# Reordering the first three stages of an eight-layer kernel: weights ahead of x, squares on ScalarE, weight copies on GpSimd, the next layer's weights behind the first rows

## The chip, the cores and the metric

The kernel runs on one core of one Trainium2 chip. The metric is the device time of one execution in microseconds (us), as the median of several runs. A core has a matmul engine (TensorE, PE in the profile; its weight loads are PEld), a vector engine (VectorE, DVE), a scalar and activation engine (ScalarE, ACT), a general engine (GpSimd, POOL) and a queue engine (SyncE, SP). Each runs its own instructions in program order and waits on semaphores for the others. SP, ACT and POOL ask for DMA transfers; an instruction that asks for one takes its place in that engine's order.

## The reference, cut to what matters

Eight layers, attention and feed-forward in turn, each `x = layernorm(x + layer(x))` on x of 8 × 256 × 256, fp32. The change touches the first three:

```python
# layer 0, attention: rotary positions, 16 query heads of 16, 4 key heads
q, k, v = x @ wq, x @ wk, x @ wv            # causal softmax(q k') v @ wo
...
# layer 0, feed-forward: 32 experts of 128 in 4 groups; each token takes 2 groups, 8 experts
scores = sigmoid(x @ gate_w.T)
... # the 2 best groups by (scores + bias), the 8 best experts in them
cw = normalised scores of those * 2.5
x_lat = x @ fc1_w.T
h = relu2(x_lat @ w1[e].T) * cw[:, e]       # relu2(x) = relu(x) ** 2
routed = sum_e(h @ w2[e].T) @ fc2_w.T
shared = relu2(x @ shared_up_w.T) @ shared_down_w.T
return shared + routed
...
# layer 1, attention: 16 heads of 128; q and k are normalised (rms) and scaled by gq and gk
```

## The kernel before, in words

The layers are eight phases in a row: attn0, ffn0, attn1, ffn1, attn2, ffn2, attn3, ffn3. x stays on chip in eight tiles X0 to X7 (256 tokens each) and transposed in four blocks xT of 512 tokens. In the first phases the order of instructions on PE, DVE, ACT and POOL is the order of the program (a hand-made schedule, `manual_schedule(engines=COMPUTE)` in `tile_layers`): python generators for pieces of work are stepped in turn, and each `yield` marks a place where another piece may be put in between. In ffn0, SP is not part of that order before the change.

**Start.** `Model.__init__` asks for the identity and for X0 to X7, even ones on SP and odd ones on ACT (L74 to L77), then for the mask `tri` (L80). `attn0_load` (L229) asks on SP, behind them, for wq in two halves, wk, wv, wo, then the rotary tables tq, ck, sk and delta. The first product of attn0 is x·wk in `project` (L279), behind the transposes of X (L145); VectorE makes kh from it with ck and sk (L288).

**attn0** (L241). A loop over eight batches (L478): maxima, spread, weights and finish of each, with pieces of other work put in at `fill` (L455 to L466): the projections of the coming block, and `beside`, the sort of ffn0's first token group, which starts at batch `NB - 2` of `NB = 8` (L488). Block 0 of ffn0's shared expert (`between`) fills the last batch.

**ffn0** (L1197). The tokens are two groups. `ffn0_sort` (L950) makes gate scores, the two groups of experts of each token, its place in a list sorted by expert group, and the eight weights, into the tile `lat` (L1036), and scatters the rows of `lat` by an indirect DMA on POOL (L929), 16 of them, into `lrows` in memory, two between `yield`s (L1040 to L1044). `ffn0_experts` (L1075) then takes 19 tiles of 128 rows a group: `fetch` loads two tiles `xg` from `lrows` (L1087, SP), `turn` copies the eight experts' first weights of that tile's expert group into `wc` (L1096 to L1101: an index read into ScalarE's register, then a copy of 128 × 1024) and transposes `xg` (L1103, copied as `xTg` by VectorE, L1105). `up` multiplies four experts (L1111), takes relu on ACT (L1116) and the square on POOL (`hg`, L1118); `down` multiplies with the second weights (L1128) and sums with the tokens' weights on DVE (`yg`, L1137 and L1139), and stores the tile (`louts`, L1141). Two halves make a tile: up of half s, then down of half s − 2. Meanwhile another generator is stepped once a half: for group 0 the sort of group 1, for group 1 `ffn0_combine` (L1156) of group 0, which gathers on POOL (L1167), adds, multiplies with fc2 (L1188), adds to x, and normalises (`normed`, L181; transposes of X in `norm_done`, L145).

Between attn0 and the tiles stand blocks 1 and 2 of the shared expert (`ffn0_shared`, L1046: up L1054, relu on ACT L1059, square on DVE L1060, down L1067, sum L1072); block 3 stands between the two groups' tiles. ffn0's second weights `f0_w2` are asked for as ffn0 begins (L1203; w_f_w in the profile), behind attn1's six weight loads of 1 MB (w_a_wq, w_a_wk, w_a_wv) and the two vectors gq and gk of 0.5 KB, which `open_weights` asks for on SP as the phase ffn0 opens.

**attn1** (L1247) first makes `gqk = gq * gk` on DVE (L1256), then works in units of a batch and four heads, its order written out in a list of `at(...)` calls; k's transposes (L1320) wait for its normalisation (L1295).

Of the kernel before, what the change touches and what calls it, by code (L numbers as in the profile page):

```python
# [18 lines left out]
P = 128  # L19
# [20 lines left out]
class Model:  # L40


    def __init__(self, ctx, tc, ins, out):
        self.tc, self.nc, self.ins, self.out = tc, tc.nc, ins, out
        nc = self.nc
        self.const = ctx.enter_context(tc.tile_pool(name="const", bufs=1, side="left"))
        self.small = ctx.enter_context(tc.tile_pool(name="small", bufs=4, side="left"))
        self.psum = ctx.enter_context(
            tc.tile_pool(name="psum", bufs=2, space=bass.MemoryType.PSUM)
        )  # L50
        self.n_ev = 0
# [26 lines left out]

        self.tri = c.tile([P, 2 * P], F32, name="tri")
        nc.scalar.dma_start(out=self.tri, in_=ins["c_tri"])  # L80
# [3 lines left out]
        for j in range(4):  # L84
            nc.vector.tensor_copy(self.maskA[:, j, :], self.tri[:, P:])
# [3 lines left out]
        nc.gpsimd.memset(self.nhalf, -0.5)  # L89


    def ps(self, tag):
        return self.psum.tile([P, 512], F32, tag=tag, name=f"ps_{tag}")
# [17 lines left out]
        else:  # L111
            self.nc.scalar.copy(out, in_)

    def load(self, pool, name, shape, split=1):
        t = pool.tile(list(shape), F32, name=f"w_{name}", tag=f"w_{name}", bufs=1)
        src = self.ins[name]
        if split == 1:
            self.nc.sync.dma_start(out=t, in_=src)
        else:
            step = shape[1] // split  # L120
            for i in range(split):
                s = slice(i * step, (i + 1) * step)
                self.nc.sync.dma_start(out=t[:, s], in_=src[:, s])
        return t

    def load_row(self, pool, name, n):
# [101 lines left out]

    def attn0_load(self, pool):  # L229
        return dict(  # L230
            wq=self.load(pool, "a0_wq", [P, 2, 512], split=2),
            wk=self.load(pool, "a0_wk", [P, 2, 256]),
            wv=self.load(pool, "a0_wv", [P, 2, 64]),
            wo=self.load(pool, "a0_wo", [P, 2, D]),
            tq=self.load(pool, "c_tq0", [P, T]),
            ck=self.load(pool, "c_ck0", [P, T]),
            sk=self.load(pool, "c_sk0", [P, T]),
            delta=self.load(pool, "c_delta", [P, 4]),
        )

    def attn0(self, w, act, start=False, beside=None, between=()):  # L241
# [236 lines left out]
        for b in range(NB):  # L478
            nxt = None
            if b == 0 or b % 2 == 1:  # L480
                drain()
                if (b + 3) // 2 < NBLK:
                    ahead.append(project((b + 3) // 2))
            if b + 1 < NB:
                nxt = maxima(b + 1)
            else:
                ahead.append(between)
            if b == NB - 2 and beside:  # L488
                sorting.append(beside)
# [12 lines left out]
            ends.append(finish(b))  # L502
            prev = nxt
# [446 lines left out]
    def ffn0_sort(self, w, g, act, keep, tag="a"):  # L950
# [87 lines left out]
            )  # L1038
        yield
        self.sorted0[g] = slots, expert  # L1040
        rows = self.scatter(self.lrows[g], slots, lambda t, k: lat[:, t, k, :])
        for i, _ in enumerate(rows):
            if i % 2 == 1:
                yield  # L1044

    def ffn0_shared(self, w, blk, act, tags=("hs", "relu"), bufs=2):  # L1046

# [3 lines left out]
        for m in range(4):  # L1051
            pu = self.ps("a" if m % 2 else "s")
            for c in range(2):
                nc.tensor.matmul(  # L1054
                    pu, w["up"][:, c, m * P : (m + 1) * P], xT[:, c, :],
                    start=(c == 0), stop=(c == 1),
                )
            relu = act.tile([P, BLK], F32, tag=tags[1], name="relu")
            nc.scalar.activation(relu, pu, AF.Relu)  # L1059
            nc.vector.tensor_tensor(hs[:, m, :], relu, relu, ALU.mult)  # L1060
            yield
        for i in range(2):
            y = self.ps("o").rearrange("p (t d) -> p t d", t=2)
# [11 lines left out]
    def ffn0_experts(self, w1, w2, g, act):  # L1075
# [17 lines left out]
        def turn(j):  # L1093
            if j % 2 == 0:
                fetch(j + 4)
            e = nc.scalar.value_load(expert[0:1, j : j + 1], min_val=0, max_val=3)  # L1096
            wc[j] = act.tile([P, 8, P], F32, tag="wc", name="wc", bufs=2)
            nc.scalar.copy(
                wc[j].rearrange("p e f -> p (e f)"),
                w1[:, bass.ds(e, 1), :].rearrange("p o f -> p (o f)"),  # L1100
            )  # L1101
            pt = self.ps("a")[:, :P]
            nc.tensor.transpose(pt, xg[j][:, :P], self.ident)  # L1103
            xT[j] = act.tile([P, P], F32, tag="xTg", name="xTg", bufs=3)
            nc.vector.tensor_copy(xT[j], pt)  # L1105

        def up(s):
            j, half = divmod(s, 2)
# [6 lines left out]
            relu = act.tile([P, BLK], F32, tag="rl", name="rl", bufs=3)  # L1115
            nc.scalar.activation(relu, ps, AF.Relu)  # L1116
            h[s] = act.tile([P, BLK], F32, tag="hg", name="hg", bufs=3)
            nc.gpsimd.tensor_tensor(h[s], relu, relu, ALU.mult)  # L1118

        def down(s):  # L1120
            j, half = divmod(s, 2)
# [34 lines left out]
    def ffn0_combine(self, w, g, keep):  # L1156
# [6 lines left out]
        for t in range(2 * n + 1):  # L1163
# [32 lines left out]

    def ffn0(self, w, act, keep, temp, sort, start=False):  # L1197

# [13 lines left out]
        for blk in (1, 2):  # L1212
            for i, _ in enumerate(self.ffn0_shared(w, blk, act)):
# [33 lines left out]
    def attn1(self, w, act, beside, then, start=False):  # L1247
# [179 lines left out]
        for n in range(len(units) + 2):  # L1427
# [28 lines left out]
            at(0, "values", 1)  # L1456
            at(0, "turned", "q", 1)
            at(1, "weights", 1)
            if 0 <= n - 2 and units[n - 2].g == 3:
# [599 lines left out]
def tile_layers(ctx: ExitStack, tc: tile.TileContext, ins, out, phases):  # L2059
# [21 lines left out]
        stack[i] = (s, load(pool, *args))  # L2081

    open_weights(0)
    left = []
    for i, name in enumerate(phases):
        m.last = i == len(phases) - 1
        with tc.tile_pool(name=f"act{i}", bufs=2, side=sides[i % 2]) as act:
            if not m.last and name != "attn1":
                open_weights(i + 1)
            w, start = stack[i][1], i == 0  # L2090
            with tc.manual_schedule(engines=COMPUTE) if name in MANUAL else ExitStack():
                if name == "attn0":
                    beside, between = None, iter(())
                    if not m.last:
# [2 lines left out]
                        between = m.ffn0_shared(wn, 0, act, ("qT", "kh0"), bufs=3)  # L2097
                    m.attn0(w, act, start, beside, between)
                elif name == "ffn0":
                    left = m.ffn0(w, act, kept[i], m.temp, left, start=start)  # L2100
                elif name == "attn1":

                    def then(i=i):
# [140 lines left out]
```

## Time and profile before

| | us |
|---|---|
| median of 3 runs (lowest to highest) | 2634.99 (2633.07 to 2637.95) |
| the profiled execution | 2582.73 |
| its span | 2580.8 |
| PE busy in the span | 2234.2 (87%) |
| DVE, ACT, POOL busy | 1454.7, 1019.0, 935.0 |
| attn0, until its last product | 0 to about 274.7 |
| end of attn0 to the first up of ffn0's tile 0 | 274.7 to 318.7 |
| ffn0's tiles of group 0 | 318.7 to 424.1 |
| block 3 of the shared expert | 424.1 to 438.3 |
| ffn0's tiles of group 1 | 438.3 to about 538 |
| attn1's first unit, until its loop is full | about 538 to 560 |

The profile is of one execution. A group's line reads: line of the kernel, engine, operation, output <- input by the program's names, shapes, count | busy time, mean ns of one | idle time of the engine just before these instructions, and what released it. A line of the timeline has start, duration, engine and operation, and in square brackets how long the engine stood idle before it and who released it; SPq is a DMA that SP asks for. In the view by stretches the columns are explained in its head line; PEclk is the granted TensorE clock as a share of full speed. In the profile `w_a_`, `w_f_` and `w_c_` are weights of attention, feed-forward and constants.

### The profile page before, as it was taken

Reading aid. Unit: us, or ns where it says so; the run is one execution under the profiler, and the core shown is the slowest. Engines: PE = TensorE matmul, PEld = TensorE weight load, DVE = VectorE, ACT = ScalarE, POOL = GpSimd, SP = SyncE. Lnnn points to the kernel's source line nnn. Section 1 sums busy time; section 2 is a strip of 40 time slices with the busy share of each in tenths; the row PEclk is TensorE's granted clock in tenths of the full one; section 3 lists DMA queues with packets and bytes.
Section 4 is the critical chain, followed back from the end, with each engine's and each line's share of the span. In section 5 each row is a group of like instructions: output and inputs, shape, how many; then the busy total and the mean of one; then the engine's idle time right before and its main releaser. Section 6 shows DMA issues by size and latency. Waiting matters only on the chain. (4 is left out here: it accounts for less than half of the span.)

```text
span 2580.8 us, 36064 instructions
## 1 busy us (share of the span) xinstructions
PE 2234.2 (87%) x12016; PEld 1518.6 (59%) x12016; DVE 1454.7 (56%) x3651; ACT 1019.0 (39%) x2909; POOL 935.0 (36%) x1637
## 2 busy tenths in 40 slices
PE   8998788889999999999999999998878777668890
PEld 4554577856666665666664555555555554457780
DVE  3565485755445445445455444556888878635453
ACT  1223143435435445445442112221666756634450
POOL 1222246544334233233313221000566656824415
PEclk9998899999999999999999999999989988789995
DMA  5000401110000100000080011002000000156653
GB/s 155 1 1 1 156 24 43 33 46 5 3 5 8 46 1 1 1 1 1 1 271 1 1 49 50 1 0 89 13 2 1 1 1 15 40 137 195 194 182 97
DMA packets 92306, 120.74 MB, mean 47 GB/s; under 512 B 9757, under 2 KB 79582, under 8 KB 91102
## 3 DMA queue, kind: packets, MB, share of 16 engines
q1 hardware_dynamic: 82702, 96.15, 11.8%
q0 software_dynamic: 8192, 21.11, 2.6%
q8 instruction: 100, 1.64, 0.3%
q10 hardware_dynamic: 1232, 1.18, 0.1%
q14 instruction: 80, 0.66, 0.1%
HBM read 67.53 MB, written 50.88 MB: 46 GB/s over the span
## 5 line engine op out<-in xcount | busy, mean ns | idle before, releaser
L1363 POOL TENSOR_SCALAR p<-p,rs 128x128 f32<-128x128 f32 (+1 forms) x256 | 104.2, 424 | 293.1 <-DVE rs L1361 282.1
L1353 ACT ACTIVATE p<-ps_s,nm,rq 128x128 f32<-128x128 f32 (+1 forms) x256 | 127.9, 506 | 148.4 <-DVE nm L1351 148.3
L137 POOL TENSOR_SCALAR rsq<-bnmv 128x2 f32<-128x2 f32 x64 | 13.7, 213 | 456.7 <-DVE bnmv L175 449.2
L1281 ACT ACTIVATE sq<-ps_a 128x512 f32<-128x512 f32 x126 | 76.0, 603 | 226.4 <-PE ps_a L1273 210.4
L638 ACT ACTIVATE e<-ps_a,nm 128x128 f32<-128x128 f32 (+1 forms) x256 | 105.8, 435 | 111.2 <-DVE nm L635 92.2
L1282 DVE TENSOR_REDUCE ssk<-sq 128x4 f32<-128x512 f32 x64 | 43.8, 686 | 174.5 <-ACT sq L1281 174.5
L680 POOL TENSOR_SCALAR v<-e,r,nmd 128x128 f32<-128x128 f32 (+1 forms) x256 | 135.9, 542 | 10.0
L1273 PE MATMUL ps_a<-w_a_wq,xT 128*128 128x512 f32 x256 | 123.4, 605 | 10.8 <-DVE k L1295 8.3
L697 PE MATMUL ps_t<-ident,v 128*128 128x128 f32 x384 | 70.3, 320 | 68.2 <-DVE qT L576 31.4
L672 DVE SCALAR_TENSOR_TENSOR e<-e,c 128x128 f32<-128x128 f32 (+1 forms) x256 | 106.2, 465 | 34.8 <-POOL c L659 34.6
L1946 PE MATMUL ps_a<-w_f_gup,xTg 128*128 x504 | 111.7, 346 | 14.7 <-DVE xTg L1940 6.8
L1273 PE MATMUL ps_a<-w_a_wv,xT 128*128 128x512 f32 x256 | 120.5, 593 | 0.0
L1273 PE MATMUL ps_a<-w_a_wk,xT 128*128 128x512 f32 x248 | 116.5, 593 | 0.0
L1282 DVE TENSOR_REDUCE ssq<-sq 128x4 f32<-128x512 f32 x64 | 43.9, 686 | 128.8 <-ACT sq L1281 128.8
L1401 PE MATMUL ps_o<-w_a_wo,attT 128*128 128x256 f32 x512 | 111.8, 379 | 0.0
L1139 DVE SCALAR_TENSOR_TENSOR yg<-ps_t,xg,yg 128x128 f32<-128x128 f32 x266 | 93.1, 350 | 26.5 <-PE ps_t L1128 17.9
L1118 POOL TENSOR_TENSOR hg<-rl 128x512 f32<-128x512 f32 x76 | 79.0, 1043 | 79.9 <-ACT rl L1116 79.6
L638 ACT ACTIVATE e<-ps_s,nm 128x128 f32<-128x128 f32 (+1 forms) x256 | 106.8, 453 | 0.0
L1401 PEld LDWEIGHTS ps_o<-w_a_wo,attT 128*128 128x128 f32 x512 | 96.8, 190 | 12.7
L1128 PE MATMUL ps_t<-w_f_w,hg 128*128 x608 | 87.2, 290 | 18.2 <-POOL hg L1118 8.4
L697 PEld LDWEIGHTS ps_t<-ident,v 128*128 128x128 f32 x384 | 50.5, 164 | 88.7 <-POOL nmd L677 44.9
L1340 PE MATMUL ps_s<-kT,qT 128*128 128x256 f32 (+1 forms) x512 | 100.1, 329 | 0.0
(402 smaller groups left out, 6142.5 us busy)
## 6 DMA issues: line engine op xcount, KB each, us to landing
rows<-zero SPq DMA_DIRECT2D x42, 384.0 KB, 4.4
xg<-rows SPq DMA_DIRECT2D x42, 384.0 KB, 3.8
outs<-yg SPq DMA_DIRECT2D x42, 384.0 KB, 4.2
w_f_gup<-in_f_gup SPq DMA_DIRECT2D x8, 768.0 KB, 10.0
w_f_w<-in_f_w SPq DMA_DIRECT2D x8, 512.0 KB, 10.4
w_f_down<-in_f_down SPq DMA_DIRECT2D x8, 384.0 KB, 9.2
w_f_up<-in_f_up SPq DMA_DIRECT2D x5, 512.0 KB, 7.2
lrows<-zero SPq DMA_DIRECT2D x12, 204.0 KB, 5.4
```

The costliest lines, as they stand in the source:

```text
L638: nc.scalar.activation(e[:, s, j * nk : (j + 1) * nk], sc[s][:, j, :], AF.Exp, bias=nm[:, s, j : j + 1], scale=1.0, accum_out=sums[:, s, j ...
L672: nc.vector.scalar_tensor_tensor(d[:, s, h, :], u.e[:, s, h, 1, :], u.c[:, s, h : h + 1], d[:, s, h, :], ALU.mult, ALU.add,)
L680: nc.gpsimd.tensor_scalar(u.v[:, s, h, :], d[:, s, h, :], u.r[:, s, h, 0:1], nm[:, s, h : h + 1], ALU.mult, ALU.add,)
L697: nc.tensor.transpose(ps[:, s, c, :], x, self.ident)
L1139: nc.vector.scalar_tensor_tensor(acc[j], y, c, acc[j], ALU.mult, ALU.add)
L1273: nc.tensor.matmul(ps, self.xt(u.b, t, c), w[which][:, c, u.cols], start=(c == 0), stop=(c == 1),)
L1282: nc.vector.tensor_reduce(out, sq, AX.X, ALU.add)
L1340: nc.tensor.matmul(sc[:, j, :], u.qT[:, h0 + j, qc * P : (qc + 1) * P], u.kT[:, h0 + j, 0:nk], start=(j == 0), stop=False,)
L1353: nc.scalar.activation(u.p[qc][:, h0 + j, :], sc[:, j, :], AF.Exp, bias=nm[:, j : j + 1], scale=r[:, j : j + 1], accum_out=u.sums[qc][:, h ...
L1363: nc.gpsimd.tensor_scalar(u.p[qc][:, j, :], u.p[qc][:, j, :], ri[:, j : j + 1], 1.0, ALU.mult, ALU.mult,)
L1401: nc.tensor.matmul(y[:, t, :], attTs[b][:, h, t * P : (t + 1) * P], w["wo"][:, h, :], start=(h == 0), stop=(h == 15),)
L1946: nc.tensor.matmul(ps, xT[j][:, c, :], w["gup"][:, bass.ds(er[j], 1), c, :].rearrange("p o f -> p (o f)"), start=(c == 0), stop=(c == 1),)
```

## The change

At the start only X0 and X1 are asked for, then attn0's weights (wk first; ck, sk, tq on the ACT queue), then the mask and the rest of x. The sort of group 0 starts one batch earlier in attn0, and yields after each scatter. The squares of ffn0 (shared and experts) go to ACT, the copy `wc` with its index read to POOL, the copy `xTg` to ACT. `ffn0_combine` has one `yield` more for each batch. In ffn0 the sort of group 1 is made during block 2 of the shared expert instead of behind it; attn1's weights are asked for there too, by `then()`, behind the tile generator's first step; and SP is part of the written order in ffn0. In attn1 the first unit's two `values` (4 matmuls each) come earlier.

```diff
@@ Model.__init__
-        for b in range(NB):
-            (nc.sync if b % 2 == 0 else nc.scalar).dma_start(
-                out=self.X[b], in_=ins["x"][b].rearrange("(t p) d -> p t d", p=P)
-            )
+        self.load_x(0, 2)
...
+    def load_rest(self):
+
+        self.nc.scalar.dma_start(out=self.tri, in_=self.ins["c_tri"])
+        for j in range(4):
+            self.nc.vector.tensor_copy(self.maskA[:, j, :], self.tri[:, P:])
+        self.load_x(2, NB)
...
@@ attn0_load
         return dict(
+            wk=self.load(pool, "a0_wk", [P, 2, 256]),
+            ck=self.load(pool, "c_ck0", [P, T], eng=self.nc.scalar),
+            sk=self.load(pool, "c_sk0", [P, T], eng=self.nc.scalar),
             wq=self.load(pool, "a0_wq", [P, 2, 512], split=2),
-            wk=self.load(pool, "a0_wk", [P, 2, 256]),
+            tq=self.load(pool, "c_tq0", [P, T], eng=self.nc.scalar),
...
@@ attn0
-            if b == NB - 2 and beside:
+            if b == NB - 3 and beside:
                 sorting.append(beside)
@@ ffn0_sort
-        rows = self.scatter(self.lrows[g], slots, lambda t, k: lat[:, t, k, :])
-        for i, _ in enumerate(rows):
-            if i % 2 == 1:
-                yield
+        yield from self.scatter(self.lrows[g], slots, lambda t, k: lat[:, t, k, :])
@@ ffn0_shared
-            nc.vector.tensor_tensor(hs[:, m, :], relu, relu, ALU.mult)
+            nc.scalar.activation(hs[:, m, :], relu, AF.Square)
@@ ffn0_experts
-            e = nc.scalar.value_load(expert[0:1, j : j + 1], min_val=0, max_val=3)
+            e = nc.gpsimd.value_load(expert[0:1, j : j + 1], min_val=0, max_val=3)
...
-            nc.scalar.copy(
+            nc.gpsimd.tensor_copy(
...
-            nc.vector.tensor_copy(xT[j], pt)
+            nc.scalar.copy(xT[j], pt)
...
-            nc.gpsimd.tensor_tensor(h[s], relu, relu, ALU.mult)
+            nc.scalar.activation(h[s], relu, AF.Square)
@@ ffn0_combine
                 self.normed(b, r, *m)
                 yield
+                yield
                 self.norm_done(b)
@@ ffn0
                 if blk == 2 and i == 3:
                     for _ in sort:
                         pass
+                    sort = self.ffn0_sort(w, 1, temp, keep)
                 if blk == 2 and i == 4:
                     next(tiles)
-        sort = self.ffn0_sort(w, 1, temp, keep)
+                    then()
@@ attn1, the order of the units
             at(0, "scaled", 1)
+            if n == 0:
+                at(0, "values", 0)
+                at(0, "values", 1)
...
-            at(0, "values", 0)
+            if n > 0:
+                at(0, "values", 0)
...
@@ tile_layers
     open_weights(0)
+    m.load_rest()
...
-            if not m.last and name != "attn1":
+            if not m.last and name not in ("ffn0", "attn1"):
                 open_weights(i + 1)
...
+            engines = COMPUTE | {mybir.EngineType.SP} if name == "ffn0" else COMPUTE
+            with tc.manual_schedule(engines=engines) if name in MANUAL else ExitStack():
...
+                    then = partial(open_weights, i + 1) if not m.last else list
+                    left = m.ffn0(w, act, kept[i], m.temp, left, then, start=start)
```

More of the change, by code (lines that the diff above doesn't have):

```diff
@@ L73, in __init__ @@
         nc.sync.dma_start(out=self.ident, in_=ins["c_ident"])
-        for b in range(NB):
-            (nc.sync if b % 2 == 0 else nc.scalar).dma_start(
-                out=self.X[b], in_=ins["x"][b].rearrange("(t p) d -> p t d", p=P)
-            )
+        self.load_x(0, 2)
         self.tri = c.tile([P, 2 * P], F32, name="tri")
-        nc.scalar.dma_start(out=self.tri, in_=ins["c_tri"])
         self.identb = c.tile([P, P], BF16, name="identb")
@@ L83, in __init__ @@
         self.maskA = c.tile([P, 4, P], BF16, name="maskA")
-        for j in range(4):
-            nc.vector.tensor_copy(self.maskA[:, j, :], self.tri[:, P:])
         self.one32 = c.tile([P, 32], F32, name="one32")
@@ L89, in __init__, with load_x @@
         nc.gpsimd.memset(self.nhalf, -0.5)
+    def load_x(self, first, end):
+        for b in range(first, end):
+            (self.nc.sync if b % 2 == 0 else self.nc.scalar).dma_start(
+                out=self.X[b], in_=self.ins["x"][b].rearrange("(t p) d -> p t d", p=P)
+            )
+    def load_rest(self):
[3 more added lines that the diff above has]
+        self.load_x(2, NB)
     def ps(self, tag):
@@ L112, in copy, with load @@
             self.nc.scalar.copy(out, in_)
-    def load(self, pool, name, shape, split=1):
+    def load(self, pool, name, shape, split=1, eng=None):
+        eng = eng or self.nc.sync
         t = pool.tile(list(shape), F32, name=f"w_{name}", tag=f"w_{name}", bufs=1)
@@ L117, in load @@
         if split == 1:
-            self.nc.sync.dma_start(out=t, in_=src)
+            eng.dma_start(out=t, in_=src)
         else:
@@ L122, in load @@
                 s = slice(i * step, (i + 1) * step)
-                self.nc.sync.dma_start(out=t[:, s], in_=src[:, s])
+                eng.dma_start(out=t[:, s], in_=src[:, s])
         return t
@@ L230, in attn0_load @@
         return dict(
+            wk=self.load(pool, "a0_wk", [P, 2, 256]),
+            ck=self.load(pool, "c_ck0", [P, T], eng=self.nc.scalar),
+            sk=self.load(pool, "c_sk0", [P, T], eng=self.nc.scalar),
             wq=self.load(pool, "a0_wq", [P, 2, 512], split=2),
-            wk=self.load(pool, "a0_wk", [P, 2, 256]),
+            tq=self.load(pool, "c_tq0", [P, T], eng=self.nc.scalar),
             wv=self.load(pool, "a0_wv", [P, 2, 64]),
             wo=self.load(pool, "a0_wo", [P, 2, D]),
-            tq=self.load(pool, "c_tq0", [P, T]),
-            ck=self.load(pool, "c_ck0", [P, T]),
-            sk=self.load(pool, "c_sk0", [P, T]),
             delta=self.load(pool, "c_delta", [P, 4]),
@@ L1193, in ffn0_combine, with ffn0 @@
                 yield
+                yield
                 self.norm_done(b)
                 yield
-    def ffn0(self, w, act, keep, temp, sort, start=False):
+    def ffn0(self, w, act, keep, temp, sort, then, start=False):
         w2 = self.load(act, "f0_w2", [P, 32, P], split=4)
@@ L1452, in attn1 @@
             step()
-            at(0, "values", 0)
+            if n > 0:
+                at(0, "values", 0)
             at(1, "scores", 1, 2)
             at(0, "turned", "q", 0)
-            at(0, "values", 1)
+            if n > 0:
+                at(0, "values", 1)
             at(0, "turned", "q", 1)
@@ L2087, in tile_layers @@
         with tc.tile_pool(name=f"act{i}", bufs=2, side=sides[i % 2]) as act:
-            if not m.last and name != "attn1":
+            if not m.last and name not in ("ffn0", "attn1"):
                 open_weights(i + 1)
             w, start = stack[i][1], i == 0
-            with tc.manual_schedule(engines=COMPUTE) if name in MANUAL else ExitStack():
+            engines = COMPUTE | {mybir.EngineType.SP} if name == "ffn0" else COMPUTE
+            with tc.manual_schedule(engines=engines) if name in MANUAL else ExitStack():
                 if name == "attn0":
@@ L2099, in tile_layers @@
                 elif name == "ffn0":
-                    left = m.ffn0(w, act, kept[i], m.temp, left, start=start)
+                    then = partial(open_weights, i + 1) if not m.last else list
+                    left = m.ffn0(w, act, kept[i], m.temp, left, then, start=start)
                 elif name == "attn1":
```

## The prediction

> **What bounds the kernel now.** I read the page first (PE is busy 87% of the span), then the eight stretches that hold the changed code: busy time of each engine, PE clock, DMA share, GB/s.
>
> ```profile
> core 0: us, PE busy (x) PEld busy (x) DVE busy (x) ACT busy (x) POOL busy (x), PEclk, DMA share, GB/s
> 0.00:26.50 26.50, 16.36 (x48) 8.83 (x48) 5.93 (x14) 1.87 (x2) 3.38 (x11) 1.00 0.93 307
> 274.70:318.70 44.00, 31.71 (x99) 20.23 (x99) 17.93 (x62) 6.41 (x10) 18.16 (x18) 0.87 0.62 229
> 318.70:424.10 105.40, 84.54 (x665) 80.45 (x664) 76.74 (x300) 44.73 (x61) 55.74 (x56) 0.95 0.12 33
> 438.30:542.30 104.00, 91.43 (x679) 83.11 (x677) 76.88 (x216) 42.38 (x58) 55.09 (x58) 0.95 0.11 28
> ```
>
> PE idles about 10 us of 26.5 at the start (1), 12 of 44 between attention and the first expert tile (2), 21 of 105 in group 0's tiles (3) and 13 of 104 in group 1's with the head of attn1 (4). What ends the idle time is in the timelines and the groups of 318.7 to 542.3:
>
> ```profile
> 12.08 2.90 PE L279 MATMUL ps_t<-xT,w_a_wk 128*128 128x512 f32 x3 [4.28 <-DMA w_a_wk<-in_a_wk]
> ...
> 280.38 7.79 SPq L123 DMA_DIRECT2D w_f_w<-in_f_w  x4
> 310.99 1.91 SPq L1087 DMA_DIRECT2D xg<-lrows  x4
> ...
> 313.32 0.45 PE L1103 MATMUL ps_a<-ident,xg 128*128 128x128 f32 x1 [5.93 <-DMA xg<-lrows]
> ...
> 545.94 1.08 PE L1320 MATMUL ps_t<-ident,k 128*128 128x128 f32 x4 [4.22 <-DVE k L1295]
> ```
> ```profile
> L1139 DVE SCALAR_TENSOR_TENSOR yg<-ps_t,xg,yg 128x128 f32<-128x128 f32 x266 | 93.1, 350 | 26.5 <-PE ps_t L1128 17.9
> L1128 PE MATMUL ps_t<-w_f_w,hg 128*128 x608 | 87.2, 290 | 18.2 <-POOL hg L1118 8.4 <-DVE yg L1139 5.2 <-DVE r_fi L853 2.4
> L1118 POOL TENSOR_TENSOR hg<-rl 128x512 f32<-128x512 f32 x76 | 79.0, 1043 | 79.9 <-ACT rl L1116 79.6
> L1116 ACT ACTIVATE rl<-ps_s 128x512 f32<-128x512 f32 x76 | 45.4, 597 | 120.1 <-PE ps_s L1111 110.4 <-POOL hg L1118 5.9 <-POOL rsq L137 3.6
> L1098 ACT COPY wc<-w_f_w 128x1024 f32 x37 | 38.7, 1045 | 3.2 <-issue 0.5 <-ACT rl L1116 0.4
> L1105 DVE COPY xTg<-ps_a 128x128 f32<-128x128 f32 x37 | 10.4, 282 | 4.8 <-PE ps_a L1103 4.8
> L145 PE MATMUL ps_t<-ident,X 128*128 128x128 f32 x16 | 3.5, 301 | 6.1 <-DVE X L181 6.1
> ```
>
> The two expert loops wait for POOL's squares, for DVE's yg, and for X at L181. PE's own work per tile is 16+16 matmuls in 3.69 us at full clock.
>
> **Part by part, against the profiled execution (2582.73; span 2580.8).**
>
> *Start.* wk is now asked for right behind X0, no longer behind all of x (2 MB) and both halves of wq. In the trace X0 lands at 5.83 and the first xT is copied by 7.68 (DVE L110); wk's 256 KB at the stretch's 307 GB/s land 0.85 after X0. So L279 starts near 7.7 instead of 12.08. DVE's four mask casts (9.68 now) wait for tri, which stands behind ck, sk and tq: 0.5 MB on that queue with as much beside it, 3.3 us behind X0, lands near 9.1; the first kh can't come before 7.7+2.9 = 10.6: just hidden, about 1 if not. The rest of x is needed one batch each 30 us (248/8) and is hidden. −4.4 (−2 to −6).
>
> *Sort one batch earlier, end of attn0.* The same DVE work a batch of 30 us earlier, beside PE that is 94% busy there (232.94 of 248.2). Ends: −2 (it leaves the tail, where lat is late by it) to +3 (it stands before the last batch's softmax on DVE, in order). Taken: +1.5, between the two and nearer to the second, since PE follows DVE in that tail.
>
> *Up to tile 0.* lat is done at 288.4 now; the 16 scatters then run 287.7 to 309.5, and xg (310.99) waits for all. Started one batch earlier, the sort has its last eighth and the squares of L1060 (four of 0.69 ahead of lat) out of DVE's way: lat about 8 earlier, 280.4; scatters (16 × 1.265 = 20.2) to 300.6, xg asked for at 302 and landed at 304 (2.6 from issue). One scatter a step instead of two only changes which instructions they stand between. ACT's added squares, 8 × 0.6, lie beside its 6.4 of 44. f0_w2 (L1203) still waits for the end of attention (274.8) and lands near 281; its first use is at 308: hidden. On PE the first up of tile 0 comes at about 308.5 instead of 318.68, and the gate matmuls of group 1, of which 24 of 32 stood inside the tiles (3.3 us), are done before it: −13.5 if nothing else is late.
>
> *The new wait.* attn1's weights, six of 1 MB, go on SP directly behind the first three xg, at about 303.3, then gq and gk, then the fourth xg (needed by tile 3, near 327 with the wait below, landed by 322) and the louts, which nobody awaits before the gathers. DVE's order in the changed kernel is: gate copies, 16 MAX8, **gqk = gq × gk, then the first yg**. Before, gqk (L1256) stood at 301.39 between two squares and waited for nothing. Queued behind it are all yg; these free ps_t, for which PE's down matmuls wait. When does gk land? Before, the same list was asked for from 274.81; wv's median is 15.6 us after 277.1, that is 18 us after the first. So 303.3+18.2 = 321.5. DVE gets there at about 312.3 (308.5 and one half tile) and stands 9.2 us; PE, with its buffers full, from about 315.6. *Rule:* the Trainium skill, "DMA: Bandwidth & Descriptors", section "Queues, rings and completion order", says that each of the sixteen engines takes its descriptors in ring order, but that completion is not in order of issue: a small load may be complete before an earlier large one; how long before, it does not say. Row: the 64 KB asked for behind four 512 KB loads took 7.8 us. With the most that the rule allows the wait is 0 (2592 in the end); by the row it is the full 9.2. I take the row, and keep 0 for rival B.
>
> *Group 0's tiles.* Removed from POOL: hg 1.04 × 2 a tile; from ACT: wc 1.05 and its register load 0.49; from DVE: xTg 0.28. Added to ACT: two squares at 0.6 (the row of L1116) and xTg 0.28; to POOL: the copy of 1024 and 0.49. ACT: 2.25 → 2.7 a tile, under PE's 3.69. POOL's price of a one-input copy is in no row; near rows: POOL affine_select takes 0.424 at 256 and 0.643 at 512 elements, so 1.08 at 1024; hg's own two-input rate gives 2.1. *Rule:* "GPSIMD Engine Reference", 3.1 "Elementwise — side-by-side cycle accounting", states about 2.6 cycles an element, about 2.2 us here, and speaks against this move. With it a tile with two scatters costs POOL 2 × 1.265+2.2+0.49 = 5.2, 1.5 over PE: 12 us over eight tiles; with the row 4.1, 3.4 in all. I take 1.1 (affine_select has one input, as the copy has); ends 0.95 to 2.2.
> Before, to 385.7 the sort on DVE binds (5.0 us a tile), from 394 to 415 POOL at 7.0 a tile (two scatters and hg each half). The same sum for before (24 half tiles × 1.64 + 21 of sort + 3 = 63.4 from 321.5) ends at 385, as measured. (1.64 is four yg of 0.35, half an xTg and 0.1 between them; 3 the additions to X.) For after: DVE is free at 321.6; 18 half tiles × 1.5 (no xTg) + 18.7 of sort (2.3 of it ran ahead) + 1.5 = 47 → 369; the other 20 halves at 1.95 (half of 3.69, and the 3.4 for scatters spread over them) → 408 to 410, instead of 424.1. So parts 2, 3 and the wait together −15 (−6 to −27).
>
> *Shared block 3 between (14.2).* Gathers 16 × 1.0 and wc(0) on POOL partly fit; the xg fetch of group 1 behind the last louts lands +4.3, needed +6.9: 0.
>
> *Group 1.* Waits shown in the rows for both groups: hg 8.4, yg 5.2, X 6.1. X's wait goes with the one added step of the combine (12 a batch × 4 = 48 against 46: one normalisation runs past the tiles). PE and DVE have about 77 to 80 us of work, so 84 to 86 instead of 97.7: −12 (−6 to −15; the low end if the clock of 0.95 and yg stay as they are).
>
> *attn1's head.* Values (2 × 4 matmuls × 0.6) fill the 4.22 wait for k: −2.5 (0 to −4).
>
> Sum: −4.4+1.5−15−12−2.5 = −32.4: 2550.3 in the profiled execution. The median runs are 2.02% above it (2634.99/2582.73): 2550.3 × 1.0202 = **2602**.
>
> **Rivals.**
> A, as above, gqk bites: 2602. For it: the order on DVE, the 7.8 us row.
> B, gq and gk land early: 9.5 more, 2592. For it: each is 0.5 KB, and the rule above. Against: they have six megabytes ahead of them on the same queue, at 419 GB/s by the trace's DMA view.
> C, the loops stay bound elsewhere: eight yg of 0.35 are 2.8 a tile, and with the sort's 20 they are DVE's work as before; only 10.4 of xTg leaves, over both groups. Idle PE time then moves from hg to yg. There remain the start (4.4), about 8 of the 13.5 before tile 0, and 2.5: −15, 2619.
> D, slower: POOL's wc copy becomes the bound of both loops. A tile costs POOL 0.49+c, in eight tiles 2.53 more. 38 tiles lose c−3.2 each, the eight 2.53 more: to eat 32.4 and lose 5.6 beyond, 38(c−3.2)+20.2 = 38, c = 3.7. From c = 3.5 it decides. Every near row and the page say 2.2 or less. At c = 3.8: 2646.
> E, no change: the six megabytes move at half the rate beside scatters, xg and louts, so that gk lands 15 later than I take it (−32.4+15), and the loops are as in C (another 15): 2632.
>
> **How the numbers follow.** A measurement tells 0.2% (5.3 us) from no change. A 0.55, B 0.20, C 0.18, D 0.03, E 0.04: faster 0.93, same 0.04, slower 0.03. Low end: B's −42, 3 for group 1's better end and 5 for group 0's: −50, 2584; about 0.05 lies below. High end: C's 2619, which A's worse ends (start 2.4, tail 1.5, group 1 6, head 2.5: 2615) don't pass; half of C, D and E, 0.16, lie above.
>
> **What would show it.** L279 near 7.7; lat near 280 and xg near 302; DVE idle for 9 us before gqk, released by a load, and PE behind it until about 322; POOL's wc copy near 1.1 us; group 1 in 85 us, with neither hg nor X among PE's waits; the 4.22 before k's transposes gone. Wrong if that copy is over 2 us, if gqk does not wait, or if the idle of PE in the loops moves to yg instead of going.

## The result, and the profile after

| | before | after |
|---|---|---|
| median of 6 runs each (lowest to highest) | 2635.62 us (2633.07 to 2638.2) | 2614.78 us (2610.6 to 2616.84) |
| ratio, with its 95% interval | | 0.9919 (0.9906 to 0.9932) |
| the profiled execution, its span | 2582.73, 2580.8 | 2616.84, 2615.1 |

The change gains 20.8 us. The forecast was 33 (2602, range 2584 to 2619): the direction and the range held, but the forecast gain was 1.6 times the measured one.

The two profiled executions must not be subtracted. They are from chips of one type but of two speeds. The kernel before takes 2639 on the chip of the first four experiments, called A here, and 2578 and 2579 on the two chips of the other eight, called B. The result (2635.62) is put to A and the first profile (2582.73) to B by these levels; their chips are not on record. In traces of the changed kernel, 61 us of the difference lie in the last layer's expert stage (294.8 on A, 234.2 on B), in code that the change doesn't touch. Ratios below are always to the kernel before on the same chip. There is no trace of the kernel before on A, so its stages can be compared on one kind of chip only on B; where A is set beside B, the text says so. Even on one kind of chip, places in the trace move between executions of one kernel: the first scatter of the kernel before came at 287.68 and 285.21 on B, that of the changed kernel at 282.27 and 284.41 on A. A shift of 2 us in one trace shows nothing by itself.

Here are the stretches of the changed kernel that answer to the four shown before (start, between attention and tile 0, the tiles of group 0, those of group 1), with the same columns, on A:

```profile
0.00:24.68 24.68, 15.57 (x48) 8.56 (x48) 5.92 (x14) 1.87 (x2) 3.37 (x11) 1.00 0.90 304
...
277.20:319.30 42.10, 34.45 (x128) 23.59 (x127) 7.77 (x17) 11.94 (x20) 18.53 (x20) 0.88 0.56 206
319.30:408.00 88.70, 76.37 (x629) 73.26 (x628) 70.14 (x278) 51.38 (x97) 33.64 (x35) 0.96 0.17 51
...
422.70:513.60 90.90, 81.65 (x668) 76.41 (x667) 69.16 (x188) 49.89 (x95) 30.14 (x33) 1.00 0.12 31
```

Set beside the first profile, which is from B, the start is 1.8 shorter, not 4.4. The stretch to tile 0 has hardly lost length, though PE has more work in it (128 matmuls instead of 99): tile 0 begins at 319.3 (before 318.7). The tiles take 88.7 and 90.9 instead of 105.4 and, without the head of attn1, 99.8. The groups of both tile loops, answering to those shown before, and below them the weight loads of the down matmuls, of the kernel before and after:

```profile
L1144 DVE SCALAR_TENSOR_TENSOR yg<-ps_t,xg,yg 128x128 f32<-128x128 f32 x266 | 93.0, 350 | 13.6 <-PE ps_t L1133 2.9 <-PE ps_s L1116 1.1 <-DVE yg L1144 0.3
L1133 PE MATMUL ps_t<-w_f_w,hg 128*128 x608 | 83.6, 281 | 9.6 <-DVE yg L1144 5.1 <-DVE r_fi L861 2.0 <-DVE m L229 0.7
L1123 ACT ACTIVATE hg<-rl 128x512 f32<-128x512 f32 x76 | 47.9, 630 | 2.4
L1103 POOL COPY wc<-w_f_w 128x1024 f32 x36 | 37.3, 1039 | 77.2 <-PE ps_s L1116 77.0
L153 PE MATMUL ps_t<-ident,X 128*128 128x128 f32 x15 | 2.5, 284 | 5.5 <-DVE yg L1144 5.5
```
```profile
L1128 PEld LDWEIGHTS ps_t<-w_f_w,hg 128*128 128x128 f32 x608 | 78.5, 202 | 23.4 <-POOL hg L1118 13.7 <-issue 9.6
...
L1133 PEld LDWEIGHTS ps_t<-w_f_w,hg 128*128 128x128 f32 x608 | 75.1, 194 | 14.5 <-DVE yg L1144 5.5 <-ACT hg L1123 3.8 <-issue 3.3
```

hg is gone from what PE's matmuls wait for (8.4 before), and their weight loads wait 3.8 for it instead of 13.7. yg stays at 5.1 in sum, but it has moved: 4.8 of it in group 0 (2.1 before) and 0.4 in group 1 (3.1 before). POOL's copy takes 1.04, near the 1.1 that the forecast took from the row of another one-input operation. It waits 77.0 for its buffer; the tiles' weight loads wait for it once, for 2.3. X is gone from the waits of the transposes (L153), and yg stands in its place, 5.5 where X was 6.1.

Three single stops of the changed kernel, from its timelines of PE and DVE on A (start, duration, what ran, idle time before it and who ended it):

```profile
11.05 3.39 PE L287 MATMUL ps_t<-xT,w_a_wk 128*128 128x512 f32 x4 [3.94 <-DMA w_a_wv<-in_a_wv]
...
252.32 0.73 PE L373 MATMUL ps_a<-qT,kT 32*128 32x512 f32 x1 [2.84 <-DVE r_te L928]
...
303.46 0.70 PE L1072 MATMUL ps_o<-w_f_down,hs 128*128 128x256 f32 x2 [2.71 <-ACT hs L1065]
```
```profile
325.08 0.16 DVE L1263 TENSOR_TENSOR gqk<-w_a_gq,w_a_gk 128x1 f32<-128x1 f32 x1 [1.04 <-DMA w_a_gk<-in_a_gk]
```

The first product waits 3.94; the stop in the second line, in attn0's last batch, is new; the third is PE waiting for a square on ScalarE; and gqk, for which the forecast set 9.2, waits 1.04. The experiments take these one by one.

### The profile page after: what moved, and what is told of

Read it like the earlier page. It is cut to its first block, busy times and chain, and to the rows that moved or that the text cites. A ratio compares the mean times of both kernels' runs of the same rounds, so it can differ in the third digit from the quotient of the medians.

```text
span 2615.1 us, 35980 instructions
## 1 busy us (share of the span) xinstructions
PE 2245.8 (86%) x12016; PEld 1522.2 (58%) x12016; DVE 1433.7 (55%) x3597; ACT 1043.8 (40%) x3001; POOL 891.6 (34%) x1599
## 4 chain that ended last, share of the span: by engine, by line
PE 25%; DVE 11%; POOL 7%; issue 3%; ACT 2%; DMA 1%; another core or an unknown queue 1%; POOLq 0%; SPq 0%; DVEq 0%; ACTq 0%
PE ps_a L1958 4%; DVE e L680 2%; PE ps_a L1579 2%; PE ps_o L1977 2%; PE ps_s L1579 2%; POOL v L688 2%; PE ps_o L1830 2%; PE ps_a L1783 2%; PE ps_s L1783 2%; DVE nm L643 1%; DVE nmd L684 1%; POOL yk L2019 1%; PE ps_t L1950 1%; DVE bnst L182 1%; POOL rows L937 1%
## 5 line engine op out<-in xcount | busy, mean ns | idle before, releaser
L145 POOL TENSOR_SCALAR rsq<-bnmv 128x2 f32<-128x2 f32 x64 | 13.7, 214 | 516.3 <-DVE bnmv L183 508.9
L1958 PE MATMUL ps_a<-w_f_gup,xTg 128*128 x504 | 119.2, 363 | 40.8 <-DVE xTg L1952 20.8
L1958 PEld LDWEIGHTS ps_a<-w_f_gup,xTg 128*128 128x128 f32 x504 | 88.4, 210 | 53.0 <-issue 28.5
L2019 POOL DMA_INDIRECT yk<-outs,r_slots x64 | 62.2, 973 | 108.3 <-DMA outs<-yg 89.9
```

What stands on the lines that cost most here:

```text
L1958: nc.tensor.matmul(ps, xT[j][:, c, :], w["gup"][:, bass.ds(er[j], 1), c, :].rearrange("p o f -> p (o f)"), start=(c == 0), stop=(c == 1),)
```

## The experiments

Theory of the forecast: the earlier sort brings the scatters forward, gqk's wait takes most of that back, the engine moves speed up both loops. The rival that the trace suggested: the engine moves carry the gain alone, and the earlier sort costs more than it brings. There are twelve runs, the first four on A, the other eight on B.

**The changed kernel again (A).** No edit.

> The changed kernel once more. About 2614 in the median, 0.992 of before. In its first trace ScalarE waited 5.1 and 1.6 us for the second and third of block 2's up products in the shared expert (near 297 to 305), though the records have those products done by 300.3, and PE then stood 2.7 and 2.2 us for the squares. Theory 1 (it belongs to this order of work): the wait is there again, and the first up of tile 0 is again near 319. Theory 2 (chance of one execution): it is gone, and tile 0 starts near 314.

Measured: 2615.2, ratio 0.9913 (0.9897 to 0.9928). The wait without a named releaser is there again (from here on, the late word: an engine that waits for a product of PE goes on only microseconds after the product's end in PE's timeline): ScalarE waits 3.7 for the second product of block 2, PE 4.3 for its square, and tile 0 begins at 322.4. Theory 1, on this chip; the third run of the kernel says more.

**The engine moves alone (A).** The kernel before with

```diff
-            nc.vector.tensor_tensor(hs[:, m, :], relu, relu, ALU.mult)
+            nc.scalar.activation(hs[:, m, :], relu, AF.Square)
-            e = nc.scalar.value_load(expert[0:1, j : j + 1], min_val=0, max_val=3)
+            e = nc.gpsimd.value_load(expert[0:1, j : j + 1], min_val=0, max_val=3)
-            nc.scalar.copy(
+            nc.gpsimd.tensor_copy(
-            nc.vector.tensor_copy(xT[j], pt)
+            nc.scalar.copy(xT[j], pt)
-            nc.gpsimd.tensor_tensor(h[s], relu, relu, ALU.mult)
+            nc.scalar.activation(h[s], relu, AF.Square)
```

> The kernel before with only the four moves between engines (squares to ScalarE, wc with its index read to GpSimd, xTg to ScalarE); loads, order and sort as before. Theory 1 (the tile loops' gain is the engines' doing): group 0's tiles 105.4 to about 95, group 1's 99.8 to about 92, so -18: 2617. Theory 2 (the gain comes from the order: sort earlier, gate products ahead of the tiles, weights later): the loops stay within 3 us each of before, 2629 or more.

Measured: 2617.0, 0.992 (0.9906 to 0.9935), beside 2615.2 for the changed kernel. So on A the four moves give all but a microsecond or two of the gain: Theory 1 in the sum, but not in the place. Equal sums hide unequal stages. Tile 0's first product, with the engine moves alone:

```profile
307.17 1.05 PE L1111 MATMUL ps_s<-xTg,wc 128*128 128x128 f32 x8
```

That is 12 earlier than the 319.3 of the whole change. From there to group 1's first product it takes 113.0, the whole change 103.4, and the last up product of group 1 ends at 508.3 and 508.1. On A, what the rest of the change wins inside group 0 is lost again ahead of tile 0.

The moves also do something that the forecast ascribed to the earlier sort. These are the first scatters on POOL, of the kernel before, of the engine moves alone, and of the changed kernel without its engine moves (below):

```profile
285.21 1.24 POOL L929 DMA_INDIRECT lrows<-lat,r_slots  x1 [9.36 <-DMA w_a_wk<-in_a_wk]
```
```profile
277.33 1.24 POOL L929 DMA_INDIRECT lrows<-lat,r_slots  x1 [4.80 <-DVE lat L1036]
```
```profile
286.49 1.24 POOL L937 DMA_INDIRECT lrows<-lat,r_slots  x1 [2.04 <-DMA w_f_w<-in_f_w]
```

(The first and third lines are from B, the second is from A.) With VectorE freed of the shared squares, lat is ready 8 earlier, with the sort at its old place; on B, in the run with the sort at its old place (below), it is 6 earlier, of which 1.6 come from the start. With the sort a batch earlier and the engine moves undone it is not earlier at all.

**gq and gk ahead of the weights (A).**

```diff
-        w = {x: self.load(pool, f"a1_{x}", [P, 2, 2048], split=2) for x in ("wq", "wk", "wv")}
-        w["gq"] = self.load(pool, "a1_gq", [P, 1])
-        w["gk"] = self.load(pool, "a1_gk", [P, 1])
+        w = {x: self.load(pool, f"a1_{x}", [P, 1]) for x in ("gq", "gk")}
+        for x in ("wq", "wk", "wv"):
+            w[x] = self.load(pool, f"a1_{x}", [P, 2, 2048], split=2)
```

> The changed kernel with gq and gk asked for ahead of the six weight loads instead of behind them. Theory 1, as predicted (gqk's wait costs 9): 2605. Theory 2 (in the trace after, VectorE came to gqk 1.0 us before gk landed, because the tiles began late for other reasons): 2613 to 2615, no wait at gqk and nothing else moved.

Measured: 2618.1, 0.9924 (0.9911 to 0.9937): no gain, theory 2 in the main. On A the tiles begin so late that gk is there. But the edit also moved gqk forward in VectorE's order, to 311.3, ahead of the sort's work.

**X3, X5, X7 on SP (A).**

```diff
-            (self.nc.sync if b % 2 == 0 else self.nc.scalar).dma_start(
+            (self.nc.sync if b % 2 == 0 or b > 1 else self.nc.scalar).dma_start(
```

> The changed kernel with X3, X5, X7 asked for on SP instead of ScalarE. In the trace after, the first product started at 11.05 when ScalarE had copied the second xT at 10.4 to 11.0: ScalarE was issuing these loads until 9.1 and loading its table until 10.4. Theory 1: that queue is the whole wait; the first product starts near 8, -3: 2611. Theory 2 (wk or the mask is what ends the wait): start unchanged, 2614.

Measured: 2613.7, 0.99 (0.9885 to 0.9916). The difference to the changed kernel beside it, 1.5, is within the scatter of runs; the trace is clear. ScalarE's timeline after, then PE's with the edit:

```profile
4.09 5.00 ACTq L88 DMA_DIRECT2D X<-in_x  x3
9.12 1.28 ACT L119 ACT_TABLE_LOAD   x1 [9.12 <-DMA X<-in_x]
10.41 0.58 ACT L119 COPY xT<-ps_t 128x512 f32<-128x512 f32 x1
```
```profile
7.75 5.61 PE L287 MATMUL ps_t<-xT,w_a_wk 128*128 128x512 f32 x8 [0.68 <-ACT xT L119]
```

The three loads of x hold ScalarE until 9.09; behind them stand the table load and the copy of the second xT, to 10.99; PE starts at 11.05. The releaser named there (wv) belongs to another product; the trace of the changed kernel again names ScalarE's xT at this place (3.65). Without the three loads PE starts at 7.75, the forecast's 7.7.

**The kernel before again (B).** No edit.

> The kernel before once more, for its trace. In every trace of this kernel's kin taken since, PE's word that a product is done reaches ScalarE and VectorE about 5 us late near 290 to 305 and in the last layer (waits without a named releaser, 27 to 37 us in each of two groups there); in the first trace of before there are none, and it took 2583 where the median runs take 2635. Theory 1 (a matter of the occasion, not of the change): they are there now, ffn3's experts take about 290 instead of 237, the profiled time is near 2635. Theory 2 (the change brings them): none, 2583.

Measured: 2578.0, beside 2578.3 for the kernel before. The run was on B and has no late words there, so neither theory is settled: whether the kernel before has them on A stays unknown.

**The sort at its old place (B).**

```diff
-            if b == NB - 3 and beside:
+            if b == NB - 2 and beside:
```

> The changed kernel with the sort of group 0 begun at batch NB - 2 again, as before. Theory 1 (the earlier sort costs attn0's last batch 4 to 5 us and does not bring lat earlier, since the square that left VectorE frees the tail by itself): attn0 ends near 268, lat is done near 277, xg is asked for near 299; but then VectorE comes to gqk near 309 and waits some 8 us for gk (asked for near 305, landed near 318): 2612 to 2615 together. Theory 2 (the earlier sort is what brings the scatters forward, as predicted): lat near 288, 2622.

Measured: 2545.1, 0.9867 (0.9853 to 0.9881), to be set against 0.9896 for the changed kernel on B. attn0 ends at 270.7 (275.6 with the earlier sort), the first scatter is at 278.9 (280.6), tile 0's first product at 307.5 (309.2). VectorE then waits 5.3 for gk. By the medians the earlier sort costs about 7 us (the two intervals just part, 0.9881 and 0.9882), and it moves no scatter forward: theory 1, a little better than it said.

**The same with gq and gk ahead (B).** Both edits above.

> As sort_late, with gq and gk asked for ahead of the six weights. Theory 1: the wait at gqk of sort_late is gone and its 8 us with it: 2605 to 2607. Theory 2 (the scatters' end or the sort on VectorE binds, not gqk): as sort_late within 1.5.

Measured: 2547.4, 0.9883 (0.9867 to 0.9898): no better than without the new load order, and theory 1 missed. The trace says why: with the earlier load gqk came to stand ahead of block 2's sum in VectorE's order, and there it waited just as well:

```profile
302.42 0.16 DVE L1263 TENSOR_TENSOR gqk<-w_a_gq,w_a_gk 128x1 f32<-128x1 f32 x1 [17.99 <-DMA w_a_gk<-in_a_gk]
```

gk itself is early now, landed 2.3 after it was asked for at 300.13. But PE then stands 6.6 before the first tile's transpose, and tile 0 begins at 311.1 instead of 307.5. To have a load early isn't enough; its reader must not stand where others wait behind it.

**The shared squares on VectorE again (B).**

```diff
-            nc.scalar.activation(hs[:, m, :], relu, AF.Square)
+            nc.vector.tensor_tensor(hs[:, m, :], relu, relu, ALU.mult)
```

> The changed kernel with the shared expert's squares (hs) on VectorE again, the experts' squares left on ScalarE. Theory 1 (PE's late word comes where VectorE stands idle while GpSimd issues indirect DMAs one behind the other, as between 294 and 305 after): VectorE works there, the late words go, tile 0 begins some 4 us earlier although attn0's tail gets four squares of 0.69 more on VectorE: 2612. Theory 2 (it has to do with PE or the scatters alone): the late words stay, and the squares cost 2 to 4: 2618.

Measured: 2556.5, 0.9919 (0.9906 to 0.9932). For the late words this run says nothing, as on B there are none either way. It does price the move: first scatter at 284.3 instead of 280.6, tile 0 at 314.8 instead of 309.2, some 6 us in the ratio.

**The changed kernel a third time (B), with the last three.**

> The changed kernel a third time, beside the three below. Ratio to before 0.991 to 0.992, on a chip where before takes 2578 as on one where it takes 2635. On the former (PE's word in time) Theory 1 says: ScalarE's waits of 5 us near 300 are absent, tile 0 begins some 5 earlier, but VectorE then waits some 9 us at gqk (9.1 in hs_on_dve), so the gain is the same 21 to 24. Theory 2: without the late word the gain is 28 or more.

Measured: 2551.9, 0.9896 (0.9882 to 0.9911), a gain of 27.5; between the two theories. Without the late words tile 0's first product is at 309.2 (forecast 308.5), and then gqk waits as forecast, and PE behind it:

```profile
323.08 0.16 DVE L1263 TENSOR_TENSOR gqk<-w_a_gq,w_a_gk 128x1 f32<-128x1 f32 x1 [9.13 <-DMA w_a_gk<-in_a_gk]
```
```profile
324.76 1.47 PE L1133 MATMUL ps_t<-w_f_w,hg 128*128 x8 [4.38 <-DVE yg L1144]
```

So on A the tiles begin 10 later and hardly meet the wait; on B they begin in time and do. From tile 0's first product to group 1's it takes 110.5 on B and 103.4 on A.

**The expert list in another PSUM buffer (B).**

```diff
-        expert = yield from self.tile_experts(w, act, keep, f"f0{g}", ends, tag=tag)
+        expert = yield from self.tile_experts(
+            w, act, keep, f"f0{g}", ends, tag="o" if g == 0 else tag
+        )
```

> The changed kernel with the transposed expert list of group 0's sort put in another PSUM buffer (the one of ps_o instead of ps_a). Theory 1 (in attn0's last batch PE stands 2.8 us because its scores need the ps_a that VectorE copies the list out of, late, and then runs 6.8 us at half clock): the 2.84 wait is gone, attn0 ends 3 to 6 earlier: 4 faster than the changed kernel. Theory 2 (VectorE's chain is late anyway, and the scores' maxima wait behind it): the wait turns up one step later, no gain.

Measured: 2546.4, 0.9876 (0.986 to 0.9892), 5.6 faster than the changed kernel; the intervals just overlap, the trace is plain. PE's timeline at the place of the 2.84:

```profile
248.71 0.27 PE L926 MATMUL ps_o<-ident,r_te 128*1 128x128 f32 x1
248.92 0.69 PE L373 MATMUL ps_a<-qT,kT 32*128 32x512 f32 x1
```

There is no wait; attn0 ends at 271.3 instead of 275.6. In the changed kernel the granted clock is 0.50 from 254 to 256, behind the stop; with the edit it is 1.00 there. Theory 1: what costs attn0's last batch its time is less the amount of the sort's work on VectorE than one small transpose in a buffer of the scores. It gives back most of what the earlier sort costs: 0.9876, and 0.9867 without the earlier sort.

**The engine moves undone (B).** The changed kernel with the diff of the engine moves reversed.

> The changed kernel with its four engine moves undone (squares on VectorE and GpSimd, wc and its index read on ScalarE, xTg on VectorE): the loads, the order and the earlier sort alone. Theory 1 (the engine moves carry the whole gain, since they alone gave 0.992, and the rest is its own loss): 0.998 to 1.002. Theory 2 (both halves gain and overlap): 0.994 to 0.996.

Measured: 2569.5, 0.9967 (0.9954 to 0.9979): a gain of 10 by loads and order alone. Theory 1 (0.998 to 1.002) does not hold on B, and theory 2's band is not met either. The trace shows where 6 of the 10 come from: group 1 takes 86.8 from its first up product to its last, 92.7 before. Of the edits left, the step added to the combine is the one that alters this loop's order, so it is likely, but not shown by itself, that it gains the 6; tile 0 is not earlier (317.6; 315.9 before), attn0 ends later (280.4; 272.2). What the engine moves gain in group 1 overlaps with it: alone 87.8 (on A), both 85.2.

**A version without the three losses (B).** The changed kernel with the sort at NB − 2, x on SP, gq and gk loaded among ffn0's weights at the start, and

```diff
+                if blk == 2 and i == 1:
+                    gqk = self.gqk = self.small.tile([P, 1], F32, tag="gqk", name="gqk", bufs=1)
+                    self.nc.vector.tensor_tensor(gqk, self.gains["gq"], self.gains["gk"], ALU.mult)
```

> The changed kernel with the sort begun at NB - 2 again, X3, X5, X7 on SP, gq and gk asked for among ffn0's weights at the start, and gqk made on VectorE between two sums of the shared expert (near 290), where VectorE stands idle. Theory 1 (the earlier sort, ScalarE's queue and the place of gqk cost about 5 to 9, 3 and 5): 13 to 17 faster than the changed kernel, ratio 0.985 to 0.987. Theory 2 (the sort's work on VectorE during group 0 takes up what is won before it): within 4 of sort_late's ratio or 0.989.

Measured: 2539.5, 0.9843 (0.9828 to 0.9859): 12.5 faster than the changed kernel and 39.9 faster than before, which is theory 1 (a little under its 13 in time, a little better in ratio). PE starts at 7.82, attn0 ends at 267.4, the first scatter is at 275.7, tile 0's first product at 306.0, and group 0 takes 103.4 without the wait.

## Why the prediction was right in direction and too large

By its own steps, with the stages of the two traces from B (the kernel before again, the changed kernel a third time), where the forecast's own basis lies. The stages end at the last product of attn0, at group 1's first product, at its last down product, and at attn1's first products of q and k (554.86 and 528.86):

| step | forecast | measured |
|---|---|---|
| start | −4.4 | −1.6 |
| end of attn0 | +1.5 | +5.0, of it 0.9 of later work drawn ahead |
| to tile 0, gqk's wait, group 0, block 3 | −15 | −19.5, of it the same 0.9 |
| group 1 (end of block 3 to the last tile) | −12 | −8.8 |
| attn1's head | −2.5 | −1.1 |
| sum | −32.4 | −26.0 |

The whole spans of these two traces (2571.4 and 2548.3) differ by 23.1, so 3 of the 26 are lost again behind these stages; the medians on B differ by 27.5. Group 1 in these two traces, before and after, with the columns of the stretches:

```profile
435.80:535.50 99.70, 87.72 (x672) 81.85 (x671) 74.84 (x211) 42.38 (x58) 55.12 (x58) 0.95 0.11 29
...
419.70:510.60 90.90, 81.64 (x668) 76.40 (x667) 69.18 (x188) 49.91 (x95) 30.16 (x33) 1.00 0.12 31
```

- **Start**: "L279 starts near 7.7" failed by its place, not by its load: three x loads on ScalarE stood ahead of the copy of xT. The forecast had considered only VectorE's casts. Shown by x on SP (7.75).
- **End of attn0**: the term was +1.5 of VectorE's work, with +3 as its worst end; it is about 4 net on B (two matmuls of 0.43 of the shared expert's block 1 have moved ahead of attn0's last product), and most of that comes from a wait for a PSUM buffer that the forecast didn't consider. Shown by the other buffer (attn0 3.6 shorter, its start being 0.7 earlier).
- **Up to tile 0**: "Started one batch earlier, the sort has its last eighth and the squares of L1060 out of DVE's way: lat about 8 earlier". The first scatter came 4.6 earlier on B, not 8, and the cause was half wrong. With the engine moves in and the sort at its old place it comes at 278.9 on B (277.3 on A with the moves alone; 285.2 before); the earlier sort without the moves does nothing for it (286.5). Of the four moves the shared squares are the one on VectorE ahead of lat; put back there, they cost 3.7 (284.3 for 280.6). This is the failed step that matters: two causes were put into one sentence and not priced apart.
- **gqk**: right, 9.13 for 9.2, with gk landed 19.4 after the first weight was asked for (18.2 forecast). The rule of the Trainium skill, "DMA: Bandwidth & Descriptors", "Queues, rings and completion order", that a small load may be complete before a large one ahead of it, brought nothing here, with six megabytes ahead on the same queue; the row decided. On A the wait shrinks to 1.0 because tile 0 is late by something else. Without it (the last run) group 0 takes 103.4 instead of 110.5, so it costs 7 in that stage.
- **Group 0**: the loop is no longer bound by POOL; the wc copy took 1.04. From the Trainium skill, "GPSIMD Engine Reference", 3.1, the forecast had estimated 2.2, with 2.6 cycles an element; but the section gives that figure for an operation with two inputs. It fits hg's old two-input product (1.04 for 512 elements; 1.1 by the page's figure, an estimate) and not this copy, which has one input. The forecast was right to go by the row of affine_select.
- **Group 1**: "X's wait goes with the one added step": it went, and a wait for yg of 1.83 a batch came for X's 1.73 (L153 above: the transposes now stand where VectorE has eight yg ahead of them). Most of the gain that remains goes with the clock (the two lines above): it is 1.00 instead of 0.95, and PE is busy 81.6 instead of 87.7 with nearly the same matmuls. What raised the clock was not tested. The forecast's 97.7 for this stage before is 99.7 in the trace on B, and its 84 to 86 after is 90.9. From group 1's first up product to its last, the engine moves alone give 4.9 (A beside B), the loads and the order alone 5.9, and both 7.5.
- **attn1's head**: the 4.22 before k's transposes is gone, and 2.14 for q at the same place, and smaller ones, came for it.
- Rival C (2619) was nearest in number to the result, and by luck: it was wrong in mechanism. The loops did gain, 9 in each; what was lost was lost ahead of them. B, D and E did not occur.

The scaling by 1.0202 is wrong in form as well: the distance between the profiled execution and the medians is not spread over the kernel but sits in the last layer (below). It makes 0.6 us of the forecast.

What stays open: why the result gives 20.8 and B 27.5 (the intervals, 0.9906 to 0.9932 and 0.9882 to 0.9911, overlap a little). With the late words on A tile 0 begins 10 later than on B, but gqk's wait falls to 1.0 there, and the last up product of group 1 ends only 3 later (508.1 and 505.1). What the kernel before loses to the late words on A was not traced. The new place of attn1's loads, the added step and attn1's earlier products were not run one by one.

## What to carry to other kernels

When work is moved off an engine and other work is started earlier, price each by itself: here the first made the second needless, and the second cost 7 us on B. Before moving a step, follow each small instruction in it to the buffer it holds and to the queue it stands in: a transpose of one row in the scores' buffer, three loads on ScalarE's queue and a product of two vectors on VectorE cost some 4 us, 3 us and 7 us in their stages, and none is in a list of costly groups. A load that is placed behind big ones is judged by its smallest rider and by who stands behind that one's reader.

## What the runs showed of the hardware that was not expected

On chip A an engine that waits for a product goes on some 5 to 8 us after the product's end in PE's timeline, in some places and in all five traces taken there; in none of the nine traces from B is there such a wait at these places. ScalarE's timeline for block 2 of the shared expert, on A and, for the same kernel, on B:

```profile
302.15 0.60 ACT L1064 ACTIVATE relu<-ps_a 128x512 f32<-128x512 f32 x1 [5.08 <-remote]
```
```profile
293.95 0.60 ACT L1064 ACTIVATE relu<-ps_a 128x512 f32<-128x512 f32 x1 [0.46 <-PE ps_a L1059]
```

On A the product that it waits for stands in PE's timeline from 295.01 to 296.9 ("remote" means that no releaser fits). In the last layer the same kind of wait adds up on A, in the changed kernel, to 27.5 us in one group of VectorE and 30.5 in one of ScalarE, and the expert stage there takes 295 us against 234 on B: that is nearly all of the 63 us between the changed kernel's 2615 and 2552. In ffn0 GpSimd is issuing indirect DMAs one behind the other at that place. The idea that it takes an idle VectorE stays untested, as that run fell on B. What in the chip makes it is open, and so is whether the signal is late or PE's recorded end too early.
